# A fused patch-matching block and 5x5 convolution on one core: row tiles with the row slot outermost, and transposes one turn later

## The chip, the core and the metric

The kernel runs on one core of a Trainium2 chip. A core has a matrix engine (TensorE, PE in the profile; its weight loads are listed apart as PEld), a vector engine (VectorE, DVE), an activation engine (ScalarE, ACT), a general engine (GpSimd, POOL) and a synchronising engine (SyncE, SP) that here only issues transfers. Sixteen DMA engines move data between the on-chip memory (SBUF, 128 partitions) and the chip's main memory, or within SBUF. TensorE writes its sums to PSUM, a small memory of its own. The metric is the device time of one execution in microseconds (us), the median over several executions.

## The reference

The input x has shape 8 x 32 x 128 x 128 (images, channels, rows, columns), all float32. Layer 0 normalises x over 16 groups of channels, matches patches, and runs three rounds of a 1x1 and a depthwise 3x3 convolution over 256 channels; its result is added to x. Layer 1 normalises again and adds a 5x5 convolution of each channel with one kernel.

```python
xb = _patch_match_stack(x)            # the 8 best of 25 shifts per pixel: 32*8 = 256 channels
dct = _conv(xb, dct_w, groups=C)
h = relu(_conv(_conv(xb, w1), w2, groups=CK, pad=1))
h = relu(_conv(_conv(h, w3), w4, groups=CK, pad=1))
wiener = sigmoid(_conv(_conv(h, w5), w6, groups=CK, pad=1))
filt = _conv(wiener * dct, inv_dct_w, groups=C)
return _conv(filt, agg_w)
...
x = x + _L0_conv_ref(_gn(x), ...)
x = x + _L1_conv_ref(_gn(x), L1_conv_kernel, 1, 2)
```

## The kernel before

An image is cut into 16 strips of 8 rows, and one more step flushes the last rows, so the main loop has 17 steps for each of 8 images. A step has four turns, for i = 3, 2, 1, 0. In turn i = 1, 2 or 3, round i of the convolutions handles the strip that has come down to it; turn 0 multiplies by the dct and starts the final sums. Every turn also gathers one unit (a half width of four rows) of the stack of matched pixels: two activations build masks (sel, L616 and L617) from the indices (ib), and TensorE picks the pixels (pg, L631).

The 256 channels are split in two halves of 128. For the second half the 1x1 convolution (`pointwise_v`, pv, L670) goes to the tile tv by ACT (L678), and the depthwise 3x3 is done tap by tap: ACT does the first (L721), DVE the other eight (L724). For the first half, `pointwise_t` (p, L694) writes to the row tile t through ACT copies (L701), and `depthwise_t` (pw, L750) does the 3x3 on TensorE. To use more of the matrix rows, t holds several rows of the strip side by side in the partitions: four groups of 32 partitions are four rows, four channel groups q lie along the free dimension, and four slots hold rows at different shifts. Slots 2 and 3 are what `pointwise_t` wrote, rows 0 to 3 and 4 to 7. Slots 0 and 1 are the same rows moved by 64 partitions, and need transfers within SBUF, the doubling transfers, issued by SP: L706 copies slots 2 and 3 of the lower 64 partitions to slots 0 and 1 of the upper ones, L708 copies slot 2 of the upper ones to slot 1 of the lower, and after the depthwise step `rows_before_t` (L648) saves slot 3 of the upper partitions as slot 0 of the lower for the next strip. In turn i, p and the transfers L706 and L708 of round i come first, and the depthwise pw of round i follows in the next turn. tv has a similar transfer (L655).

The next image is prepared beside all this, in small tasks. A task is a generator that yields the name of a queue (D for work on DVE, A for ACT, P for TensorE, Q for the squares' sums), a cost, and optionally a number of turns to wait. `push` (L211) puts it in its queue with the earliest turn at which it may run; `run` (L217) runs, in the order of the queue, what is due. `now` counts turns: it is raised in `tick` (L1016), which runs the D queue up to a credit. In each turn of the main loop the order is: the pv matmuls; in turn 3 the final sums pa (L830) of the turn before; `run("P")` (L1083); in turn 0 the dct (`final_dct`, pc, and the DVE products L817, which free pc's PSUM tiles); `run("Q")`; `tick` (L1091); the second part of the final sums on DVE (L838); the eight taps; p with its transfers; pg; pw; `run("A")`.

Three tasks matter here. `costs` (L485) sums the squared differences of a quarter of the image's rows on DVE (L508 to L520, first the tile v, then dsum), transposes them on TensorE (pt, L525), and finds the eight best (L536, L537). `places` (L542) then turns the indices of the quarter into places in a table on DVE (oc, L551 to L560), yields "P" (L566), transposes them on TensorE (pi, L569), casts them on ACT (li, L571) and writes them out with four POOL transfers (idxd, L573). v (L505) and oc (L548) share one buffer: both have the tag "v" with bufs=1. An image has four quarters, i = 0 to 3.

PE, DVE and ACT run in the order in which the program is written; the order on SP and POOL, which issue the transfers, is set by a planner with a cost model.

Of the kernel before, what the change touches and what calls it, by code (L numbers as in the profile page):

```python
# [16 lines left out]
P = 128  # L17
C, K, H, W = 32, 8, 128, 128
# [26 lines left out]
def bm3d_conv_preact(  # L45
# [16 lines left out]
    nc = tc.nc  # L62
# [54 lines left out]
    tb = [const.tile([P, 4, 4, W], F32, name=f"t{i}") for i in range(3)]  # L117
# [367 lines left out]
    def costs(b, i, sq, idx):  # L485
# [35 lines left out]
        for h in range(0, R, 4):  # L521
# [9 lines left out]
            for q in range(4):  # L531
                yield "D", 1.85
                y = 8 * i + h + q
                for rg in range(4):
# [3 lines left out]
                        idx[:, rg, y // 4, :, y % 4], mx[:, 4 * q + rg], c25  # L538
                    )
        push(places(b, idx, i))  # L540

    def places(b, idx, i):  # L542


        if i == 0:
            idxd[b] = dram.tile([4, 8, 2, K * 4, HW], U8, name=f"idxd_{b}", tag="idxd")
        yield "D", 2.6
        oc = work.tile([P, R, W + 2], F32, name=f"oc_{b}_{i}", tag="v", bufs=1)  # L548
        oc = oc.rearrange("p r w -> p (r w)")
        o, ct = oc[:, 0:256], oc[:, 256:512]  # L550
        nc.vector.tensor_copy(  # L551
            o.rearrange("p (g z) -> p g z", g=4),
            idx[:, :, 2 * i : 2 * i + 2].rearrange("p g s k y -> p g (s k y)"),
        )
        nc.vector.tensor_scalar(ct, o, 5.0, None, op0=ALU.is_ge)
        for lim in (10.0, 15.0, 20.0):
            nc.vector.scalar_tensor_tensor(ct, o, lim, ct, op0=ALU.is_ge, op1=ALU.add)
        nc.vector.scalar_tensor_tensor(o, ct, float(QW - 5), o, op0=ALU.mult, op1=ALU.add)
        o3 = o.rearrange("p (s y) -> p s y", y=4)
        nc.vector.tensor_tensor(  # L560
            o3,
            o3,
            base.unsqueeze(1).to_broadcast([P, 64, 4]),
            ALU.add,
        )
        yield "P", 0  # L566
        for h in range(2):
            pt = ps_x.tile([P, 512], F32, name=f"pi_{b}_{i}_{h}", tag="x")
            nc.tensor.transpose(pt[:, :P], o[:, h * P : (h + 1) * P], ident)  # L569
            li = work.tile([P, P], U8, name=f"li_{b}_{i}_{h}", tag="li")  # L570
            nc.scalar.copy(li, pt[:, :P])  # L571
            for f in range(2):
                nc.gpsimd.dma_start(  # L573
                    idxd[b][i, 4 * h : 4 * h + 4, f],
                    li[:, HW * f : HW * (f + 1)],
                )
        ready.add((b, i))
        if i == 3:
            ready.add(b)
# [64 lines left out]
    def rows_before_t(i, b, n):  # L644

        t = tb[i - 1]
        if n < NS:
            nc.sync.dma_start(t[0:64, :, 0], t[64:P, :, 3])  # L648
        else:
            nc.gpsimd.memset(t[0:64, :, 0], 0.0)  # L650

    def rows_before_v(i, b, n):
        v = tv[i - 1]
# [26 lines left out]
    def pointwise_t(i, b, n, lhsT, src):  # L680
        t = tb[i - 1]
        nb = 2 if n < NS else 1
        nr = 4 if n < NS else i - 1
        if n == NS and i == 1:
            nc.gpsimd.memset(t[:, :, 2], 0.0)
        else:
            for q in range(2):
                ps = ps_x.tile([P, 2, 2, W], F32, name=f"p{i}_{b}_{n}_{q}", tag="x")
                for e in range(2):
                    s = slice(C * (2 * q + e), C * (2 * q + e + 1))  # L690
                    for g in range(2):
                        rows = src(g)
                        for r in range(nr):
                            nc.tensor.matmul(  # L694
                                ps[C * r : C * (r + 1), e, :nb],
                                lhsT[:, g, s],
                                rows[:, r : r + 4 * nb - 3 : 4],
                                start=g == 0,
                                stop=g == 1,
                            )  # L700
                nc.scalar.copy(  # L701
                    t[: C * nr, 2 * q : 2 * q + 2, 2 : 2 + nb], ps[: C * nr, :, :nb]
                )
            for r in range(i - 1) if n == 0 else range(i - 1, 4) if n == NS else ():
                nc.gpsimd.memset(t[C * r : C * (r + 1), :, 2], 0.0)
        nc.sync.dma_start(t[64:P, :, 0:nb], t[0:64, :, 2 : 2 + nb])  # L706
        if nb == 2:
            nc.sync.dma_start(t[0:64, :, 1], t[64:P, :, 2])  # L708

    def depthwise_v(i, b, n):  # L710
        v = tv[i - 1]
# [18 lines left out]
        rows_before_v(i, b, n)  # L730

    def depthwise_t(i, b, n):
        t = tb[i - 1].rearrange("p q (h k) w -> p q h k w", k=2)
        nb = 2 if n < NS else 1

        pt = [
            ps_dw.tile([P, 2, 2, W], F32, name=f"pw{i}_{b}_{n}_{u}", tag=f"dw{u}")
            for u in range(2)
        ]

        nh = [2 if n < NS else (i + 1 - u) // 2 for u in range(2)]

        parts = ((1, 2), (0, 1)) if i != 2 and n < NS else ((0, 2),)
        for ka, kz in parts:
            for u in range(2):
                hi, kz = 96 if u == 0 else P, min(kz, nh[u])
                for dx in (0, -1, 1):
                    xa, xz = max(0, -dx), min(W, W - dx)
                    for j in range(4 if kz > ka else 0):
                        nc.tensor.matmul(  # L750
                            pt[u][C * j : C * (j + 1), ka:kz, :nb, xa:xz],
                            dwd[0:hi, i - 1, u, j, dx + 1],
                            t[0:hi, j, ka:kz, :nb, xa + dx : xz + dx],
                            start=dx == 0,
                            stop=True,
                            skip_group_check=True,
                        )
        yield 1
        acc = accp.tile([P, R, W], F32, name=f"acc{i}_{b}_{n}_0", tag=f"acc{i}0")
        rows = acc.rearrange("p (k e) w -> p e k w", e=4)  # L760
        for u in range(2):
            if nh[u]:
                nc.scalar.activation(  # L763
                    rows[:, u : u + 2 * nh[u] - 1 : 2, :nb], pt[u][:, : nh[u], :nb], funcs[i - 1]
                )
        rows_before_t(i, b, n)
        accs[i, b, n][0] = acc

# [265 lines left out]
    with tc.manual_schedule(engines=ORDERED):  # L1034
# [2 lines left out]
        push(mixes())  # L1037
        xbd[0] = dram.tile([P, 2, H, W], F32, name="xbd_0", tag="xbd")
        for i in range(3):
            nc.gpsimd.memset(tb[i][0:64, :, 0], 0.0)  # L1040
        for u in range(7):
            unit(gather_load, u)

# [10 lines left out]
        for s in range(len(steps) + 2):  # L1054
            if s < len(steps):
                b, n = steps[s]
# [8 lines left out]
            for i in (3, 2, 1, 0):  # L1065
# [6 lines left out]
                if live and i:  # L1072
                    src = source(i, bi, ni)
                    pointwise_v(i, bi, ni, lws[i - 1], src)
                    new_v, new_t = depthwise_v(i, bi, ni), depthwise_t(i, bi, ni)
                    accs[i, bi, ni] = [None, next(new_v)]
# [17 lines left out]
                if live and i:  # L1094
                    pointwise_t(i, bi, ni, lws[i - 1], src)
# [81 lines left out]
```

## Time and profile before

| | |
|---|---|
| median of 3 runs | 6640.18 us (6636.07 to 6641.82) |
| the profiled execution | 6645.45 us, span 6643.7 us |
| PE busy, share of the span | 6238.3 us, 94% |
| DVE busy | 5862.9 us, 88% |
| ACT busy | 5054.4 us, 76% |
| POOL busy | 3079.3 us, 46% |
| queue 1 (transfers issued by SP): packets, MB, share of the 16 DMA engines | 383568, 258.11, 17.6% |
| queue 0 (transfers issued by POOL) | 383648, 611.87, 36.9% |
| L724 (DVE taps): count, mean | 3264, 1237 ns |
| L750 (pw on PE): count, mean | 31680, 420 ns |
| granted TensorE clock, mean | 0.978 |

The profile is of one execution; its span runs from the first to the last instruction. A line of the list of waits reads: engine, tile and line that waited, what ended the wait, then the total in us, the number of waits and the longest. A line of the timeline reads: start in us, length in us, engine, line, operation, tiles written and read with their sizes, how many such instructions are merged, and in brackets the idle time of that engine just before and what ended it. A wait for several things is put down to the one that came last by the profile, which can be an unrelated transfer. Matmuls overlap, so a TensorE line's length is not a sum of its instructions' lengths.

### The profile page before, as it was taken

What the parts mean: (1) busy time and instruction counts of PE and PEld (TensorE: products, weight loads), DVE (VectorE), ACT (ScalarE), POOL (GpSimd) and SP (SyncE); (2) the same over time, 40 slices, a digit from 0 to 9 for tenths busy, and PEclk for the clock granted to TensorE, in tenths of its full rate; (3) what the DMA queues carried; (4) which work ended last, traced back from release to release, by engine and by line L of the source; (5) the groups of instructions that cost most, each with busy time, mean ns of one, the idle gap of its engine ahead of it and who ended that gap; (6) DMA issues with size and microseconds to landing.
All of it is one profiled execution on the core that took longest, in us unless ns stands there. A gap on an engine that the chain in (4) does not pass through costs nothing.

```text
span 6643.7 us, 234197 instructions
## 1 busy us (share of the span) xinstructions
PE 6238.3 (94%) x102306; PEld 3236.5 (49%) x102306; DVE 5862.9 (88%) x8828; ACT 5054.4 (76%) x6698; POOL 3079.3 (46%) x5015
## 2 busy tenths in 40 slices
PE   5898899999999999999999999999999999999997
PEld 1444455544555545544555544554445544454553
DVE  7889988999889998898989998899888999887786
ACT  5787778777787777877778877887769777687772
POOL 8354346444464343643446444464435543344334
PEclk8899999999999999999999999999999999999998
DMA  4555555656555564655646656465555655556553
GB/s 85 126 138 130 131 131 130 148 134 140 131 143 136 130 147 118 149 134 133 144 121 147 147 126 149 120 154 136 130 137 132 148 136 130 125 141 145 137 133 82
DMA packets 770751, 886.20 MB, mean 133 GB/s; under 512 B 248880, under 2 KB 614000, under 8 KB 769728
## 3 DMA queue, kind: packets, MB, share of 16 engines
q0 software_dynamic: 383648, 611.87, 36.9%
q1 hardware_dynamic: 383568, 258.11, 17.6%
q8 instruction: 805, 13.19, 0.9%
q10 hardware_dynamic: 2512, 1.25, 0.1%
q14 instruction: 218, 1.79, 0.1%
HBM read 420.60 MB, written 216.49 MB: 96 GB/s over the span
## 4 chain that ended last, share of the span: by engine, by line
PE 43%; DVE 29%; DMA 9%; ACT 8%; POOL 6%; issue 4%; SPq 0%; ACTq 0%; DVEq 0%; POOLq 0%
DVE acc L724 20%; PE pw L750 14%; PE pv L670 11%; PE p L694 9%; PE pg L631 3%; DMA t<-t 3%; POOL xtd L424 2%; DVE df L444 2%; DVE idx L537 2%; PE pc L809 2%; ACT sel L616 2%; ACT df L452 2%; DMA xf<-xbd 2%; DVE acc L817 1%; PE p L923 1%
## 5 line engine op out<-in xcount | busy, mean ns | idle before, releaser
L724 DVE SCALAR_TENSOR_TENSOR acc<-tv,dwv,acc 128x1024 f32<-128x1024 f32 (+3 forms) x3264 | 4032.3, 1237 | 240.8 <-ACT acc L721 136.8
L750 PE MATMUL pw<-t,dwd 96*32 96x254 f32 (+7 forms) x31680 | 2124.6, 420 | 51.0 <-DMA t<-t 38.4
L750 PEld LDWEIGHTS pw<-t,dwd 96*32 96x32 f32 (+1 forms) x31680 | 1088.4, 110 | 874.5 <-issue 411.2
L616 ACT ACTIVATE sel<-ib,nplace 128x1024 f32<-128x1024 uint8 x1024 | 1172.1, 1145 | 37.4 <-DMA ib<-idxd 37.4
L617 ACT ACTIVATE sel<-sel 128x1024 f32<-128x1024 f32 x1024 | 1085.7, 1060 | 32.5
L694 PE MATMUL p<-acc,lw 128*32 128x256 f32 x16768 | 1002.9, 383 | 24.7 <-ACT tv L678 23.3
L670 PE MATMUL pv<-acc,lw 128*32 128x512 f32 x8448 | 956.2, 590 | 48.7 <-DVE acc L817 43.4
L602 POOL DMA_DIRECT2D ib<-idxd x512 | 292.5, 571 | 1241.8 <-ACT sel L616 1176.2
L790 POOL DMA_DIRECT2D xf<-xbd x1088 | 651.9, 631 | 316.1 <-PE pc L809 180.1
L694 PEld LDWEIGHTS p<-acc,lw 128*32 128x32 f32 x16768 | 579.2, 111 | 437.1 <-issue 79.4
L452 ACT ACTIVATE df<-df 128x786 f32<-128x786 f32 (+2 forms) x576 | 468.6, 861 | 340.5 <-DVE df L444 337.8
L631 PE MATMUL pg<-sel,xt 120*32 120x88 f32 (+1 forms) x24576 | 616.1, 244 | 63.6 <-ACT sel L617 50.7
L631 PEld LDWEIGHTS pg<-sel,xt 120*32 120x32 f32 x24576 | 556.8, 110 | 235.0 <-ACT sel L617 70.1
L678 ACT COPY tv<-pv 128x512 f32<-128x512 f32 (+2 forms) x784 | 437.1, 579 | 305.0 <-PE pv L670 293.0
L444 DVE TENSOR_TENSOR df<-xn 128x786 f32<-128x786 f32 (+2 forms) x576 | 531.6, 973 | 81.2 <-PE pd L459 80.2
L728 ACT ACTIVATE acc<-acc 128x1024 f32<-128x1024 f32 (+3 forms) x408 | 417.3, 1023 | 241.6 <-DVE acc L724 241.3
L763 ACT ACTIVATE acc<-pw 128x512 f32<-128x512 f32 (+2 forms) x808 | 438.5, 573 | 182.7 <-PE pw L750 182.0
L670 PEld LDWEIGHTS pv<-acc,lw 128*32 128x32 f32 x8448 | 286.0, 111 | 534.1 <-issue 428.7
L701 ACT COPY t<-p 128x512 f32<-128x512 f32 x800 | 424.4, 571 | 118.0 <-PE p L694 118.0
L721 ACT ACTIVATE acc<-tv,dwv 128x1024 f32<-128x1024 f32 (+3 forms) x408 | 454.9, 1115 | 33.9 <-PE pa L830 20.6
L670 PE MATMUL pv<-xb,lw 128*32 128x512 f32 x4096 | 473.5, 596 | 0.0
L694 PE MATMUL p<-xb,lw 128*32 128x256 f32 x8192 | 468.5, 379 | 1.0 <-DVE xy L935 0.9
(155 smaller groups left out, 5932.9 us busy)
## 6 DMA issues: line engine op xcount, KB each, us to landing
ib<-idxd POOLq DMA_DIRECT2D x512, 256.0 KB, 4.1
xbd<-xb POOLq DMA_DIRECT2D x128, 1024.0 KB, 5.9
xf<-xbd POOLq DMA_DIRECT2D x960, 128.0 KB, 7.1
t<-t SPq DMA_DIRECT2D x792, 128.0 KB
t<-t SPq DMA_DIRECT2D x384, 256.0 KB
tv<-tv SPq DMA_DIRECT2D x384, 130.0 KB
xt<-xtd POOLq DMA_DIRECT2D x240, 180.0 KB, 3.7
xtd<-xl POOLq DMA_DIRECT2D x192, 96.0 KB, 3.5
```

The lines of the kernel that those rows point to most:

```text
L444: nc.vector.tensor_sub(df[:, :, ca:cz], xn[:, r0 : r0 + SR, ca:cz], xn[:, r0 + dy : r0 + dy + SR, ca + dx : cz + dx],)
L452: nc.scalar.activation(df[:, :, ca:cz], df[:, :, ca:cz], AF.Square)
L616: nc.scalar.activation(sel, ib, AF.Square, bias=nplace)
L617: nc.scalar.activation(sel, sel, AF.Relu, scale=-1.0, bias=1.0)
L631: nc.tensor.matmul(pg[C * j : C * (j + 1), :, :, xa:xz], xt[: 8 * QW, f * (NT // 2) + t], sels[j // 2][: 8 * QW, j % 2 * 2 : j % 2 * 2 + 2 ...
L670: nc.tensor.matmul(ps[C * j : C * (j + 1), :hr], lhsT[:, g, P + C * j : P + C * (j + 1)], src(g)[:, h : h + hr], start=g == 0, stop=g == 1,)
L694: nc.tensor.matmul(ps[C * r : C * (r + 1), e, :nb], lhsT[:, g, s], rows[:, r : r + 4 * nb - 3 : 4], start=g == 0, stop=g == 1,)
L721: nc.scalar.activation(acc, rows, AF.Copy, scale=tap)
L724: nc.vector.scalar_tensor_tensor(acc, rows, tap, acc, op0=ALU.mult, op1=ALU.add)
L750: nc.tensor.matmul(pt[u][C * j : C * (j + 1), ka:kz, :nb, xa:xz], dwd[0:hi, i - 1, u, j, dx + 1], t[0:hi, j, ka:kz, :nb, xa + dx : xz + dx ...
L763: nc.scalar.activation(rows[:, u : u + 2 * nh[u] - 1 : 2, :nb], pt[u][:, : nh[u], :nb], funcs[i - 1])
L790: nc.gpsimd.dma_start(xf[p : p + C, m, j0:j1], src[g, m, (h + m + 1) % 2, :, :, ya:yz])
```

## The change

In the row tiles t the slot becomes the outermost of the free dimensions: from (q, slot, column) to (slot, q, column). All accesses to t follow. What a doubling transfer moves in one partition was four pieces of one or two rows (512 or 1024 bytes) and is now one piece of four or eight rows (2048 or 4096 bytes). A depthwise matmul that takes two or four rows of one q now finds them 512 elements apart instead of 128. Apart from that, the P part of `places` waits one more turn for every image but the first.

```diff
@@ places
-        yield "P", 0
+        yield "P", 0, 1 if b else 0
@@ rows_before_t
-            nc.sync.dma_start(t[0:64, :, 0], t[64:P, :, 3])
+            nc.sync.dma_start(t[0:64, 0], t[64:P, 3])
         else:
-            nc.gpsimd.memset(t[0:64, :, 0], 0.0)
+            nc.gpsimd.memset(t[0:64, 0], 0.0)
@@ pointwise_t
-            nc.gpsimd.memset(t[:, :, 2], 0.0)
+            nc.gpsimd.memset(t[:, 2], 0.0)
...
                 nc.scalar.copy(
-                    t[: C * nr, 2 * q : 2 * q + 2, 2 : 2 + nb], ps[: C * nr, :, :nb]
+                    t[: C * nr, 2 : 2 + nb, 2 * q : 2 * q + 2].rearrange("p b e w -> p e b w"),
+                    ps[: C * nr, :, :nb],
                 )
...
-                nc.gpsimd.memset(t[C * r : C * (r + 1), :, 2], 0.0)
-        nc.sync.dma_start(t[64:P, :, 0:nb], t[0:64, :, 2 : 2 + nb])
+                nc.gpsimd.memset(t[C * r : C * (r + 1), 2], 0.0)
+        nc.sync.dma_start(t[64:P, 0:nb], t[0:64, 2 : 2 + nb])
         if nb == 2:
-            nc.sync.dma_start(t[0:64, :, 1], t[64:P, :, 2])
+            nc.sync.dma_start(t[0:64, 1], t[64:P, 2])
@@ depthwise_t
-        t = tb[i - 1].rearrange("p q (h k) w -> p q h k w", k=2)
+        t = tb[i - 1].rearrange("p (h k) q w -> p q h k w", k=2)
@@ before the first step
-            nc.gpsimd.memset(tb[i][0:64, :, 0], 0.0)
+            nc.gpsimd.memset(tb[i][0:64, 0], 0.0)
```

## The prediction

> **What bounds the kernel now.** I read the page first, then the waits of TensorE, the instructions that touch tile v, and the timeline around the work that moves.
>
> ```profile
> span 6643.7 us, 234197 instructions
> ...
> PE 6238.3 (94%) x102306; PEld 3236.5 (49%) x102306; DVE 5862.9 (88%) x8828; ACT 5054.4 (76%) x6698; POOL 3079.3 (46%) x5015
> ...
> PE 43%; DVE 29%; DMA 9%; ACT 8%; POOL 6%; issue 4%; SPq 0%; ACTq 0%; DVEq 0%; POOLq 0%
> ```
>
> Two engines share the bound: PE idles only 405 us, and DVE holds 29% of the chain. Which one binds changes from step to step, so each edit must be priced where it falls. The waits of PE hold both stalls that the change touches:
>
> ```profile
> PE pi L569 <- DVE oc L560: 63.2, 16, 20.2
> ...
> PE pv L670 <- DVE acc L817: 43.4, 25, 3.0
> PE pw L750 <- DMA t<-t: 38.4, 27, 4.0
> ```
>
> The moved transposes (pi) cost 63.2 us in 16 waits, the doubling transfers 38.4 us in 27. The question is what stands behind each. Tile v, which shares its single buffer with oc, gives the first hint, in the list of what DVE waited for:
>
> ```profile
>   PE pi L569: 2.8, 4
> ```
>
> **Part 1, the transposes one turn later.** P items run before the tick of a turn. An item left by tick N runs now in turn N+1, before tick N+1; with the extra turn it runs in turn N+2, after tick N+1. Image 0 keeps the old order; its four waits (1.2, 6.8, 20.2, 8.1) are 36.3 of the 63.2 us. What is left is 26.9: 2.0, 8.6 and 3.1 in image 1, about 2.1 in each of the six last quarters of images 2 to 7 (12.4), and 0.8 in small ones.
>
> The last quarters are worth nothing. In the timeline, during image 4, for image 5:
>
> ```profile
> 4082.96 0.42 DVE L560 TENSOR_TENSOR oc<-oc,base 128x256 f32<-128x256 f32 x1
> 4083.30 10.52 DVE L724 SCALAR_TENSOR_TENSOR acc<-tv,dwv,acc 128x1024 f32<-128x1024 f32 x8
> 4083.53 0.41 PE L569 MATMUL pi<-cst,oc 128*128 128x128 f32 x2 [2.14 <-DVE oc L560]
> ...
> 4093.74 2.47 DVE L817 TENSOR_TENSOR acc<-acc,pc 128x512 f32<-128x512 f32 x4
> 4094.47 5.34 PE L670 MATMUL pv<-acc,lw 128*32 128x512 f32 x32 [2.20 <-DVE acc L817]
> ```
>
> DVE goes from oc through eight taps to L817 without a gap, and PE waits for L817 again 11 us later. PE that skips the first 2.1 us waits 2.1 more at the second: 0 of 12.4.
>
> The third quarters turn into a loss, and it is the largest term. Quarter 2 of images 2 to 7 (and quarter 1 of image 1) has the costs of the next quarter (L508, tile v) in tick N+1, directly behind oc on DVE:
>
> ```profile
> 4003.40 0.43 DVE L560 TENSOR_TENSOR oc<-oc,base 128x256 f32<-128x256 f32 x1
> ...
> 4003.99 0.44 PE L569 MATMUL pi<-cst,oc 128*128 128x128 f32 x2
> ...
> 4004.46 1.24 DVE L508 TENSOR_TENSOR v<-dsum 128x1040 f32<-128x1040 f32 x1 [0.64 <-DMA xf<-xbd]
> ...
> 4008.41 1.23 DVE L520 TENSOR_TENSOR dsum<-dsum,v 128x1024 f32<-128x1024 f32 x1
> ...
> 4012.34 0.66 PE L525 MATMUL pt<-cst,dsum 128*128 128x128 f32 x4
> ```
>
> ```profile
> 4809.37 1.24 DVE L508 TENSOR_TENSOR v<-dsum 128x1040 f32<-128x1040 f32 x1 [0.59 <-PE pi L569]
> ```
>
> L508 starts 0.03 us after the second transpose ends (here, and in the next image, where the idle time is put down to pi): v may not overwrite oc before the transposes have read it. After the change those transposes stand in turn N+2, where L525 stands now. Per case: 4012.34 less the 0.37 us that pi gives up at its old place is 4011.97; the transposes end at 4012.41, L508 starts at 4012.44 instead of 4004.46. DVE is 7.98 us late. The other five images give the same to 0.02 us (the distances from L508 to L525 are all 7.86 to 7.88). PE stalls too: L525 needs L520, which ends 5.2 us after L508's start, so PE stands 5.2 us at L525. Behind L508 on DVE are L838 and the three runs of eight taps of that step, and none has slack: after 4004.46 the next idle time of DVE over 0.15 us comes at 4051.99, past L817 at 4045.08, for which PE waits 0.7 us (1.1, 1.8, 1.0, 1.4 and 2.0 in the others). So the whole 8.0 reaches PE: 6 x 8.0 = +47.8 us. The least would be PE's own stall, 6 x 5.2 = 31, if DVE caught up.
>
> Image 1: quarter 1 loses 6.0 us on DVE (L508 from 711.92 to 717.95), quarter 2's wait of 8.6 goes, quarter 3's 3.1 falls before a stretch in which DVE runs 30 us without a gap. DVE next idles 6.6 us in that stretch at 822. So of +6.0 and -8.6, between -1 and +5 is left; I take +2. Quarters 0 and 1 of images 2 to 7 have 53 us or more until the next v: 0. With the transposes go two li casts (0.21 us each; ACT is 76% busy) and four idxd issues (0.69 us each) on POOL, which waits 160 us for li now, with xf, ib and sq issues behind; those are loaded turns ahead, and idxd is read a quarter later, at least a step away. I put 0, and 10 us to either side.
>
> **Part 2, the layout.** Instructions on PE, ACT and POOL are as many as before. A depthwise row now lies 512 elements from the next. L694 reads rows at that distance already: 64 instructions over 256 columns issue in 3.45 us, 54 ns each; L750's 96 over 254 or 256 take 5.16, also 54 ns. Cost 0. The L701 copies write four runs instead of two, as L678 does: 579 against 571 ns, 800 times, 6 us on ACT, hidden by its 24% idle time; on the path it would be those 6. The memsets (about 0.52 us) become contiguous: 0.
>
> The transfers carry the same bytes in a quarter of the pieces: L708 and L648 64 x 2 KB instead of 256 x 512 B, L706 64 x 4 KB instead of 256 x 1 KB. From the recorded completions, issue end to last completion, median and 90th percentile:
>
> | line | pieces | us |
> |---|---|---|
> | L706 | 256 x 1024 B | 3.40, 7.31 |
> | L648 | 256 x 512 B | 3.24, 7.48 |
> | L708 | 256 x 512 B, behind L706 | 3.61, 7.42 |
> | L655 (tv) | 128 x 1040 B | 2.73, 6.48 |
>
> Twice the bytes in as many pieces cost nothing in the tail; half the pieces with the same bytes save 0.9. So the tail goes by pieces. The PE waits are L708's slowest: landing 10 to 14 us after issue in most of them, PE arriving 1 to 3 us earlier. At 2022 to 2034 L706's and L708's pieces trickle in beside an out_dram transfer that lands in 11 us, 1 KB pieces taking 106 to 158 ns (76 is their median) between 4 KB packets of some 400. A quarter of the pieces should bring these landings below 9 us. Addressable: 38.4, and the 3.1 that the view puts down to tv; less 2.6 in four waits with an L817 wait right behind; less 3.4 of the very last (4.0 us, only 3.5 after an issue); less 3.5 in five steps where DVE is soon the later one: 32. I take 85%: -27. Ends: +3 (bytes decide; 4 KB pieces hold up others, though 121,696 such packets run already) and -39.
>
> The Trainium skill (DMA: Bandwidth & Descriptors, Why small descriptors are slow) holds the penalty of small pieces to be one of HBM, not of SBUF to SBUF. By it part 2 is worth 0 and the sum is +50. The tv row says otherwise in the tail, by 0.9 us.
>
> Fewer pieces also free DMA time: q1's t packets take 14.5% of the 16 engines now. For other loads I put -2.
>
> **Sum**, against the profiled run (span 6643.7, device time 6645.5, which is 5.3 above the median of 6640.2): 47.8 + 2 - 27 - 2 = +21. Median 6661.
>
> **Rivals.**
> A. DVE's wait at v does not reach the end: PE, not DVE, is the later one there, or v's order differs. For: DVE's share is 88%, not 100. Against: no gap in DVE until L817, and PE waits there in all six. It ends faster once over 27 of the 48 us is hidden; with all hidden 6640 - 27 - 5 (image 1's wait) - 2 = 6606. Chance 0.15.
> B. The transfers land no sooner. For: an L706 piece of 1 KB takes 76 ns, tv's 1040 B 47, so bytes may bind with 64 partitions. Against: the tails above. 6640 + 50 = 6690. Chance 0.15.
> C. SP and POOL, whose order a planner sets from its own costs, are ordered differently, and xf or ib come late. Against: PE has no wait for xf. Some 15 us either way about the sum, 6645 to 6676. Chance 0.10.
>
> **How the numbers follow.** My forecast has 0.60; its own range is 6643 to 6685 (part 1 between 31 + 2 and 53, part 2 between -10 and -29). The 8 in 10 range, 6612 to 6692, takes in most of A and B. A measurement of this kernel can tell about 0.2% (13 us) from no change. Faster: 0.13 of A, 0.02 of C, 0.01 of mine, 0.16. Same: 0.16 of mine, 0.02 of A, 0.03 of C, 0.21. Slower: 0.43 of mine, all of B, 0.05 of C, 0.63.
>
> **What the profile after would show.** Part 1: DVE v L508 waiting for PE pi seven times, some 55 us in all; PE pt L525 waiting about 5 us six times for DVE dsum; PE pi's wait down to the 36 us of image 0; L817 waits of 2 to 3 us at the end of those steps. Part 2: PE pw waiting for t<-t under 10 us; t<-t as 2 and 4 KB pieces; L694 and L750 at 54 ns. I am wrong if L508 still starts within a microsecond of oc's end, or if pw's wait stays above 25 us.

## The result, and the profile after

| | before | after |
|---|---|---|
| median | 6641.44 us (6636.07 to 6652.68, 5 runs) | 6671.53 us (6665.80 to 6675.45, 5 runs) |
| ratio to before, 95% interval | | 1.0044 [1.0029, 1.0059] |
| profiled execution, span | 6643.7 us | 6673.7 us |

The change makes the kernel 0.44% slower, about 29 us. The forecast was 6661 us, slower. Lines of the code after L701 are one higher than before (L724 is now L725, L750 is L751, L817 is L818, L708 is L709).

The page of the kernel after. The first lines are the span and the busy times; then the queue that SP feeds (packets, MB, share of the 16 DMA engines), and the chain by engine:

```profile
span 6673.7 us, 234198 instructions
...
PE 6246.8 (94%) x102306; PEld 3230.4 (48%) x102306; DVE 5862.1 (88%) x8828; ACT 5051.2 (76%) x6698; POOL 3081.1 (46%) x5015
...
q1 hardware_dynamic: 157776, 258.11, 15.9%
...
PE 46%; DVE 27%; ACT 10%; DMA 7%; POOL 6%; issue 4%; SPq 0%; ACTq 0%; POOLq 0%; DVEq 0%
```

No engine does more work than before: the counts in the line of busy times are the same. SP's queue carries the same 258.11 MB in 157,776 packets instead of 383,568. Of the 30 us of span, 21.5 are idle time of PE (405.4 us before, 426.9 after), and 8.5 are the same matmuls taking longer (6238.3 us before, 6246.8 after). The list of waits of PE after the change says which waits are new:

```profile
PE pg L631 <- ACT sel L617: 63.0, 39, 2.3
...
PE pt L525 <- issue: 37.2, 8, 5.3
PE pi L569 <- DVE oc L560: 36.0, 4, 20.3
PE pw L751 <- DMA t<-t: 22.7, 17, 3.9
```

The wait for oc fell from 63.2 us to the 36.0 of image 0, and the wait for the doubling transfers from 38.4 to 22.7. In their place PE stands 37.2 us at pt, which was not in the list of before in this size, and 12 us more than before at pg, whose wait for sel was 50.7 us. The wait at pt is put down to "issue", that is to nothing the profile shows; the timeline below shows what it is. The list of waits of DVE after the change has one new row:

```profile
DVE v L508 <- PE pi L569: 53.9, 8, 8.1
```

It was 2.8 us before. The timeline of the kernel after, around quarter 2 of an image, the same place as the one shown for before at 4003 us:

```profile
4020.84 0.42 DVE L560 TENSOR_TENSOR oc<-oc,base 128x256 f32<-128x256 f32 x1
...
4028.75 0.44 PE L569 MATMUL pi<-cst,oc 128*128 128x128 f32 x2
...
4029.22 1.24 DVE L508 TENSOR_TENSOR v<-dsum 128x1040 f32<-128x1040 f32 x1 [7.96 <-PE pi L569]
...
4033.17 1.23 DVE L520 TENSOR_TENSOR dsum<-dsum,v 128x1024 f32<-128x1024 f32 x1
...
4034.49 1.08 PE L525 MATMUL pt<-cst,dsum 128*128 128x128 f32 x4 [5.31 <-issue]
...
4035.51 5.18 PE L694 MATMUL p<-acc,lw 128*32 128x256 f32 x64
```

Read it from the top. oc is complete at 4021.26. The transposes that read it now start 7.49 us later. v may not be written before they are done, because it lies in the same buffer, so DVE idles 7.96 us and starts L508 0.03 us after the transposes' end. L520 ends at 4034.40, and the pt transposes, which need its result, start 0.09 us later: the 5.31 us that are put down to "issue" end with dsum. Both numbers were in the forecast: 7.98 and 5.2.

The last line shows where PE's longer busy time comes from. The same 64 matmuls took 3.66 us behind the transposes of before:

```profile
4004.36 3.66 PE L694 MATMUL p<-acc,lw 128*32 128x256 f32 x64
```

In the trace the granted clock is 0.50 from 4031.8 to 4038.6 us, and 1.00 in the 11.8 us before. Each of the other five stalls of 5.3 us at pt has 6.8 us at 0.50 around its end too, in the kernel after and in e1 and e8 below. So each of the six costs PE its 5.3 us and, by the lengths of L525 (1.08 against 0.66 us) and L694, an estimated 1.9 us more here; where L694 takes 5.65 and 5.75 us, at two other stalls, it is 2.4 and 2.5.

### The profile page after: what moved, and what is told of

It is laid out like the page before. It is cut to its first block, busy times and chain, and to the rows that moved or that the text cites. A ratio compares the mean times of both kernels' runs of the same rounds, so it can differ in the third digit from the quotient of the medians.

```text
span 6673.7 us, 234198 instructions
## 1 busy us (share of the span) xinstructions
PE 6246.8 (94%) x102306; PEld 3230.4 (48%) x102306; DVE 5862.1 (88%) x8828; ACT 5051.2 (76%) x6698; POOL 3081.1 (46%) x5015
## 3 DMA queue, kind: packets, MB, share of 16 engines
q1 hardware_dynamic: 157776, 258.11, 15.9%
## 4 chain that ended last, share of the span: by engine, by line
PE 46%; DVE 27%; ACT 10%; DMA 7%; POOL 6%; issue 4%; SPq 0%; ACTq 0%; POOLq 0%; DVEq 0%
DVE acc L725 19%; PE pw L751 16%; PE pv L670 12%; PE p L694 10%; PE pg L631 4%; POOL xtd L424 3%; ACT sel L616 2%; DVE idx L537 2%; PE pc L810 2%; DMA t<-t 2%; ACT df L452 2%; DVE df L444 2%; PE pa L831 1%; DMA xf<-xbd 1%; DVE acc L818 1%
## 5 line engine op out<-in xcount | busy, mean ns | idle before, releaser
L725 DVE SCALAR_TENSOR_TENSOR acc<-tv,dwv,acc 128x1024 f32<-128x1024 f32 (+3 forms) x3264 | 4032.1, 1237 | 248.1 <-ACT acc L722 144.0
L751 PE MATMUL pw<-t,dwd 128*32 128x254 f32 (+7 forms) x31680 | 2124.6, 420 | 30.1 <-DMA t<-t 22.7
L751 PEld LDWEIGHTS pw<-t,dwd 128*32 128x32 f32 (+1 forms) x31680 | 1089.4, 111 | 854.2 <-issue 403.8
L616 ACT ACTIVATE sel<-ib,nplace 128x1024 f32<-128x1024 uint8 x1024 | 1172.4, 1145 | 34.2 <-DMA ib<-idxd 34.2
L694 PE MATMUL p<-acc,lw 128*32 128x256 f32 x16768 | 1011.3, 384 | 20.6 <-ACT tv L678 19.6
L694 PEld LDWEIGHTS p<-acc,lw 128*32 128x32 f32 x16768 | 578.0, 112 | 436.3 <-issue 81.6
L701 ACT COPY t<-p 128x512 f32<-128x512 f32 x800 | 424.1, 571 | 125.0 <-PE p L694 125.0
L694 PE MATMUL p<-xb,lw 128*32 128x256 f32 x8192 | 468.3, 380 | 3.7 <-ACT tv L678 3.7
```

The lines of the kernel that those rows point to most:

```text
L616: nc.scalar.activation(sel, ib, AF.Square, bias=nplace)
L694: nc.tensor.matmul(ps[C * r : C * (r + 1), e, :nb], lhsT[:, g, s], rows[:, r : r + 4 * nb - 3 : 4], start=g == 0, stop=g == 1,)
L725: nc.vector.scalar_tensor_tensor(acc, rows, tap, acc, op0=ALU.mult, op1=ALU.add)
L751: nc.tensor.matmul(pt[u][C * j : C * (j + 1), ka:kz, :nb, xa:xz], dwd[0:hi, i - 1, u, j, dx + 1], t[0:hi, j, ka:kz, :nb, xa + dx : xz + dx ...
```

## The experiments

Each median is of 5 to 12 executions. The ratio is to the kernel before, with its 95% interval; one per cent is 66 us.

| kernel | layout | delay | oc | out_dram pieces | median us | ratio |
|---|---|---|---|---|---|---|
| after | new | yes | shares v's | 62 rows | 6671.53 | 1.0044 [1.0029, 1.0059] |
| e8 | new | yes | shares v's | 62 | 6674.56 | 1.0041 [1.0029, 1.0053] |
| e1 | old | yes | shares v's | 62 | 6679.61 | 1.0045 [1.0030, 1.0060] |
| e2 | new | no | shares v's | 62 | 6628.55 | 0.9971 [0.9961, 0.9980] |
| e3 | new | yes | its own | 62 | 6622.37 | 0.9961 [0.9946, 0.9975] |
| e4 | new | no | its own | 62 | 6622.27 | 0.9960 [0.9946, 0.9974] |
| e11 | old | yes | its own | 62 | 6629.39 | 0.9979 [0.9968, 0.9989] |
| e5 | new, without L709 | no | shares v's | 62 | 6619.75 | 0.9955 [0.9942, 0.9968] |
| e6 | new | no | shares v's | 32 + 30 | 6602.40 | 0.9934 [0.9921, 0.9947] |
| e7 | old | no | shares v's | 32 + 30 | 6610.77 | 0.9948 [0.9935, 0.9961] |
| e9 | new | no | its own | 32 + 30 | 6604.33 | 0.9940 [0.9927, 0.9953] |
| e10 | new | yes | its own | 32 + 30 | 6603.18 | 0.9940 [0.9927, 0.9952] |

### Each part alone (e1, e2)

e1 keeps the old layout and has only the delay:

```diff
-        yield "P", 0
+        yield "P", 0, 1 if b else 0
```

> The row tiles as before, only the transposes of places one turn later. Theory (v waits in the shared buffer for the transposes): +46 us on the time before, ratio about 1.007; DVE v L508 waits some 54 us for PE pi, PE pt L525 some 5 us in seven places, PE pw waits for t<-t about 38 us as before. Rival (the layout costs the time, the delay is harmless or helps): ratio 1.000 or below, no wait of v.

e2 is the kernel after with that one line undone.

> The new layout alone, transposes where they were. Theory: 10 to 20 us faster than before, ratio 0.997 to 0.9985, since PE pw's wait for t<-t fell from 38 to 23 us in the changed kernel; v waits under 4 us. Rival (the layout costs): ratio about 1.004, like the changed kernel. Rival (the landings are worth nothing): 1.000.

Measured: the delay alone costs 0.45% (30 us) where 46 were expected, the layout alone gains 0.29% (19 us). The wait at v in e1's list of waits of DVE, and the answering ones in its list of PE:

```profile
DVE v L508 <- PE pi L569: 57.6, 8, 8.2
```

```profile
PE pw L750 <- DMA t<-t: 42.4, 27, 4.4
...
PE pt L525 <- issue: 37.0, 7, 5.3
PE pi L569 <- DVE oc L560: 36.9, 4, 20.2
```

In e2, v waits for pi only 2.9 us in all, and in its list of PE's waits the doubling transfers stand at what they are in the kernel after:

```profile
PE pi L569 <- DVE oc L560: 62.1, 13, 20.2
...
PE pw L751 <- DMA t<-t: 20.7, 16, 3.9
```

So the loss is the delay's, and the layout is a gain. But the two do not add: 30 less 19 would be +11, and the kernel after has +0.44% and, run again as e8, +0.41%, the same as the delay alone. Read the other way, the delay costs 0.70 to 0.73% (46 to 48 us) on top of the new layout, and 0.45% on top of the old. These two differ by some 18 us, little more than their uncertainty of about 15.

### Is it the shared buffer? (e3, e11, e4)

The rival to the hold at v is that the later transposes, casts and transfers of places cost the time themselves. e3 leaves the delay and the order of all work as in the kernel after, and gives oc a buffer of its own, so v no longer has to wait:

```diff
-        oc = work.tile([P, R, W + 2], F32, name=f"oc_{b}_{i}", tag="v", bufs=1)
-        oc = oc.rearrange("p r w -> p (r w)")
+        oc = work.tile([P, 512], F32, name=f"oc_{b}_{i}", tag="oc", bufs=1)
```

> The whole change, but oc has a buffer of its own, so v need not wait for the transposes. Theory: v's 54 us of waits and the 5 us waits of pt go, the time is 15 to 22 us below that of before, ratio 0.9967 to 0.998. Rival (the later transposes cost through POOL's idxd transfers or ACT's casts, not through the buffer): the time stays with the changed kernel's, ratio about 1.004.

The timeline of e3 at the same place as the one above:

```profile
3993.30 0.42 DVE L559 TENSOR_TENSOR oc<-oc,base 128x256 f32<-128x256 f32 x1
3993.67 1.24 DVE L508 TENSOR_TENSOR v<-dsum 128x1040 f32<-128x1040 f32 x1
...
4001.08 0.44 PE L568 MATMUL pi<-cst,oc 128*128 128x128 f32 x2
...
4001.35 0.60 PE L525 MATMUL pt<-cst,dsum 128*128 128x128 f32 x4
```

The transposes are as late as in the kernel after (7.36 us behind oc's end; 7.49 there), but v follows oc without a gap, pt follows pi without one, and these waits of v and pt are gone from the lists. The ratio goes from 1.0044 to 0.9961: 0.83%, 55 us, taken back by a buffer alone, and somewhat more than expected. e11 is the same pair with the old layout (e1 with oc's own buffer):

> Old layout, delay, oc in a buffer of its own: the delay without its price, and a second measure of the layout, against the kernel with new layout, delay and own buffer (0.9961). Theory (the layout is worth 0.25 to 0.3% wherever v is not held): ratio 0.9985 to 1.000. Rival (the layout is worth nothing beside the delay, as the 1.0041 and 1.0045 of the two delayed kernels suggest): 0.996 to 0.997.

From e1 to e11 it is 0.66%, 44 us, with e11 a little under its expected range. These differences carry some 12 to 14 us of uncertainty each. That the hold at v is the loss is shown; that the transposes' lateness itself costs nothing shows in e4, which has the own buffer and no delay:

> New layout and oc's own buffer, transposes where they were. Tells what the delay by itself is worth once v cannot be held. Theory (PE's waits for oc in the last quarters only move to the next wait for DVE): within 8 us of the kernel with own buffer and delay, ratio 0.997 to 0.9985. Rival (the 27 us of waits that the delay takes away are worth their length): 25 us slower than that kernel, ratio about 1.001.

e3 and e4 have the same time (0.9961 and 0.9960). PE waits 36.8 us for oc in the one and 62.0 in the other, and the 25 us between them are worth nothing: where PE skips that wait it meets a later one. Its idle time in all is no less in e3, 403.5 us against 396.6; its waits at pd for df are 53.6 us against 44.2, and at pv for L817 47.5 against 39.7. The own buffer without the delay (e2 to e4) gains 0.11%, 6 to 7 us, within the uncertainty; that part of e3's 55 us may be due to the buffer and not to the hold.

### What the doubling transfers can be worth, and what makes them late (e5, e6, e7)

e5 is e2 without the transfer L709. Slot 1 of the lower partitions stays zero, so the rows that the depthwise step reads there are left out of the sums; the number of matmuls is unchanged.

```diff
         nc.sync.dma_start(t[64:P, 0:nb], t[0:64, 2 : 2 + nb])
-        if nb == 2:
-            nc.sync.dma_start(t[0:64, 1], t[64:P, 2])
...
-            nc.gpsimd.memset(tb[i][0:64, 0], 0.0)
+            nc.gpsimd.memset(tb[i][0:64, 0:2], 0.0)
```

> New layout, transposes where they were, and the transfer of L709 (slot 2 of the upper partitions to slot 1 of the lower) left out, so that rows 2 and 3 of the lower groups are zero: what the doubling transfers can bring at most. Theory (what is left of PE pw's wait for t<-t, 20 us, is nearly all L709): that wait under 5 us, 12 to 18 us faster than the layout alone, ratio 0.994 to 0.9955. Rival (PE only waits elsewhere): ratio as the layout alone, 0.997.

Measured 0.9955, with PE's wait for these transfers almost gone:

```profile
PE pw L749 <- DMA t<-t: 4.9, 3, 4.0
```

That bounds it: of the 20.7 us that e2 still waits, taking the later transfer away altogether brings 0.16%, 10 us, and the intervals of the two overlap.

Most of the waits that remain after the change have one thing in common in the trace: beside 11 of the 17, and 15.9 of the 22.7 us, transfers of 62 output rows, out_dram<-xy, were issued. The other six have none near them. At 3665.3 us, for example, L709 was issued 13.12 us before PE's wait ends and landed 0.04 us before that, when 15 of its 16 completions had been in for 2.1 us; an out_dram transfer was issued 13.24 us before and landed 0.13 us after. Those land in 11 us, and unevenly: of the 16 completions of each, the first comes 5.1 us after the issue, the eighth 6.1, the last 11.4 (medians). e6 is e2 with those transfers cut in two, and e7 is the kernel before with the same cut:

```diff
-                for a, z in ((0, 62), (66, P)):
+                for a, z in ((0, 32), (32, 62), (66, 96), (96, P)):
```

> New layout, transposes where they were, and each output transfer of 62 rows cut in one of 32 and one of 30. Theory (the late landings of t come from the one or two DMA engines on which a 62-row transfer, 11 us to landing, ends long after the other engines): out_dram<-xy lands in 5 us or less, PE pw's wait for t<-t falls from 20 to under 8 us, ratio 0.993 to 0.996. Rival (the queues are simply full): the wait stays near 20 us, ratio 0.997 or more, since POOL issues 112 transfers more.

> The kernel before with the output transfers cut in the same way, rows of t in pieces of 512 and 1024 bytes as before. Theory (uneven engines): PE pw's wait for t<-t falls from 38 to 42 us to under 12 with the old pieces, ratio 0.994 to 0.997. Rival (the number of pieces makes the waits): the wait stays above 30 us, ratio 0.999 to 1.002.

In e2, everything about out_dram, columns: shortest, median and longest of one issue on POOL in ns, then first and last start; then who on POOL waited for those transfers, and issue to landing:

```profile
L938 POOL DMA_DIRECT2D out_dram<-xy x112: 1504/1519/1587, 1210.7 to 6154.7; - x112
...
L938 POOL DMA_DIRECT2D out_dram<-xo x8: 1502/1504/1546, 6583.8 to 6606.0; - x8
...
  POOL xy L885: 105.4, 15
  POOL xf L791: 85.4, 50
  POOL xy L890: 42.4, 14
...
DMA to landing us min/median/max: 1.9/10.8/16.2
```

The same of e6:

```profile
L938 POOL DMA_DIRECT2D out_dram<-xy x224: 561/588/637, 1210.1 to 6152.8; - x112
...
L938 POOL DMA_DIRECT2D out_dram<-xo x16: 565/583/623, 6579.0 to 6599.0; - x16
...
  POOL xy L890: 28.1, 13
  POOL xy L885: 2.5, 2
...
DMA to landing us min/median/max: 1.6/2.2/5.2
```

A part lands in 2.2 us where the whole took 10.8 (medians over all output transfers), and takes POOL 0.59 us to issue instead of 1.52. POOL itself waited 233 us for them in those three rows of e2, and waits 31 in e6. PE's wait for the doubling transfers in e6, and then in e7, which has the old small pieces:

```profile
PE pw L751 <- DMA t<-t: 8.8, 7, 3.7
```

```profile
PE pw L750 <- DMA t<-t: 16.3, 14, 4.1
```

| PE's wait at pw, us | 62 rows | 32 + 30 rows |
|---|---|---|
| old layout | 38.4 | 16.3 |
| new layout | 20.7 | 8.8 |

One profile is not exact here: the other kernels with 62 rows have 40.2 and 42.4 with the old layout and 19.2 to 26.6 with the new, and those with 32 + 30 rows and the new layout 8.3 and 10.8. The cut brought the two waits down a little less than expected (under 12 with the old layout, under 8 with the new). The landings agree: the 90th percentile of L708, from the issue's end to the last completion, is 7.42 us before, 5.62 with the cut alone (e7) and 7.16 with the layout alone (L709 in e2). So the landings were late in good part because of these output transfers, and the layout and the cut take the same waits from two sides. With the old layout the cut gains 0.52%, with the new one 0.37% more (0.9971 to 0.9934); the layout on top of the cut is worth 0.14% (0.9948 to 0.9934), half of its 0.29% alone, and the intervals of that pair overlap. Part of the cut's gain is no matter of t at all: the kernel ends with such transfers. From the start of the last issue of this line to the end of the span it takes 17.4 us in e2 (6606.0 to 6623.4) and 6.1 in e6 (6599.0 to 6605.1), 11.3 us less.

e6 has the lowest ratio of this study: 0.66% faster than before, and 1.1% faster than the change.

### The delay once more, with all of this gone (e9, e10)

e9 is e6 with oc's own buffer, e10 is e9 with the delay.

> Everything that helped, without the delay: new layout, output transfers cut in 32 and 30 rows, oc in a buffer of its own. Theory: the own buffer alone brings under 8 us, so ratio 0.992 to 0.9935, the fastest of all. Rival (the own buffer moves other things for the worse): 0.994 or more.

> The same with the transposes one turn later. Theory (with v free the delay neither helps nor harms, as between the two kernels with own buffer): within 8 us of the kernel without the delay, ratio 0.991 to 0.9945. Rival (the delay takes away 25 us of waits that count once the transfers are out of the way): 0.989.

Both come to 0.9940, and e6 without either to 0.9934, all within the uncertainty. The delay is worth nothing even where it harms nothing, and so is the buffer, to which e9's expectation had given up to 8 us.

> The changed kernel again, beside the others, since the delay alone came out as slow as the whole change. Theory (the parts add up, +0.45% and -0.29%): ratio 1.001 to 1.003. Rival (the layout is worth nothing once v is held): 1.0045 as at first.

e8, the kernel after on the chip of e5 to e7, gave 1.0041; v waited 54.9 us for pi in its profile. So the parts do not add here either, and the loss repeats.

## Why the prediction was right or wrong

**The sum** was +21 us, measured about +29, inside the forecast's own range. Its main mechanism is shown. That the number came so near is in part luck: the layout brought less than forecast, and the delay alone cost less too, so that two errors offset each other; and the sum took for granted that the two parts add, which they do not.

**The hold at v** (+47.8, and +6 in image 1, if all of it reaches the end): v waited 53.9 us in 8 places where seven and some 55 were forecast (the eighth, 0.84 us in image 0, stands before as well), 7.96 us in the one shown against 7.98 worked out, PE 5.31 at pt against 5.2. It reaches the end in full, or nearly: e3 takes back 55 us, e11 44, of which the buffer by itself may be worth some 6. Rival A, in which it did not, is out. The prediction has no term for the clock, which stands at 0.50 for 6.8 us at each of the six stalls. With it PE's own loss is an estimated 7.2 to 7.8 us at each (5.3 standing, 1.9 to 2.5 on slower matmuls) and not the 5.2 that made its low end of 31 us; how much of the 8 us comes by DVE and how much by PE is not separated.

**Image 1 and the last quarters.** The last quarters were put at 0, since DVE sets their end, and they are. The timeline of the kernel after, one quarter on:

```profile
4107.55 0.42 DVE L560 TENSOR_TENSOR oc<-oc,base 128x256 f32<-128x256 f32 x1
4107.89 10.52 DVE L725 SCALAR_TENSOR_TENSOR acc<-tv,dwv,acc 128x1024 f32<-128x1024 f32 x8
...
4118.33 2.47 DVE L818 TENSOR_TENSOR acc<-acc,pc 128x512 f32<-128x512 f32 x4
...
4119.06 1.92 PE L670 MATMUL pv<-acc,lw 128*32 128x512 f32 x16 [2.65 <-DVE acc L818]
```

One wait of 2.65 us stands where there were 2.14 and 2.20, and from oc's end to the matmuls behind L818 it is 11.09 us as before (4083.38 to 4094.47 there): nothing gained.

**The net of the delay** was forecast at some 50 us. On top of the new layout it cost 46 to 48, as forecast; alone it cost 30 (e1). If that difference is real, a gain is missing from the forecast, and the term that would have to hold it is "Quarters 0 and 1 of images 2 to 7 have 53 us or more until the next v: 0". In quarter 1 of the image shown, PE waited 0.21 us for oc, 1.28 for df and 3.67 for tv (p, L694) before the change, and 0.59 for df and 1.96 for tv after it, about 2 us less. Why is not shown. The own buffer with the delay and the old layout (e11) ends 14 us under the kernel before, which has the same sign, but no run tells the buffer's share there from the delay's; with the new layout and the own buffer the delay is worth nothing (e3 against e4). The cause of the 18 us stays open.

**Part 2** (-27, ends +3 and -39) was over-sized. The step that failed is the 85%: it took the tail of the landings to go by the number of pieces. The 1 KB pieces of 106 to 158 ns that it named at 2022 to 2034 us are the slow ones: by the packets on record half of the 1 KB pieces in that stretch took 66 ns or less. From the recorded completions, issue end to last completion, median, 90th and 97th percentile:

| transfer | before | after |
|---|---|---|
| L706, now L707 | 3.40, 7.31, 9.81 | 3.07, 7.14, 8.78 |
| L708, now L709 | 3.61, 7.42, 9.28 | 3.50, 6.96, 8.69 |
| L648 | 3.24, 7.48, 8.28 | 3.42, 6.89, 7.76 |

A quarter of the pieces took 0.2 to 0.6 us from the 90th percentile and 0.5 to 1.0 from the 97th. The slowest landings, for which PE waits, still come late: pw's wait went to 22.7 us instead of under 10. It did not stay above the 25 that was to refute the step, though in e3 it is 26.6. What made most of these landings late stood beside them in the trace, the output transfers of 62 rows (e6 and e7). The worth of the layout is 19 us alone, 0.18% (12 us) between e11 and e3, 0.14% between e7 and e6, and 1 to 3 us beside the delay. Between 0 and 20, then, and why it is least there is open. One way would be that PE, let through earlier at pw, waits for a DVE that the hold has made late; no run separates that from the uncertainty of these differences.

The page of the Trainium skill that the prediction set against the tv row (DMA: Bandwidth & Descriptors, Why small descriptors are slow) came closer than the prediction did: between parts of SBUF, pieces four times as large moved the median landing by 0.3 us at most. It isn't nothing, though: alone the layout gains 0.29% [0.20, 0.39]. So rival B, no gain from it, is out for the layout by itself, and near the truth beside the delay with the shared buffer.

What was costed at nothing stayed there: L751 and L694 issue a matmul per 54 ns in both layouts, and an L701 copy takes 571 ns in both, so the 6 us that were feared on ACT did not come. Rival C, late loads, does not show: PE has no wait for xf in its list, and ACT waits 34.2 us for ib after the change and 37.4 before it.

## What to carry to other kernels

Before a reader is moved later, look up who writes its buffer next: two tiles under one tag with a single buffer turned a free delay into 8 us of DVE, six times over, and a buffer of its own removed it. Look at the granted clock behind a new stall as well: here 5.3 us of standing came with 6.8 us at half the clock. A wait in a list is worth only what stands behind it: 25 us of waits for oc went away from e4 to e3 for no gain, while an own buffer for a wait that the list of before showed at 2.8 us decided the sign. When transfers land late, look at what else was issued in those microseconds before reshaping the transfers that are late; the list of POOL's waits of before had named it:

```profile
POOL xf L790 <- DMA out_dram<-xy: 83.3, 49, 4.4
```

Forty-nine times a load stood behind an output transfer.

## What was not expected of the hardware

A transfer of 62 partitions from SBUF to the main memory, 4 pieces of 512 bytes each, costs far more than two of 32 and 30: 1.52 us against 0.57 and 0.60 to issue on POOL, 11 us against 2.1 and 2.4 to land (e2 and e6). The queue that POOL feeds shows a difference in packets, in the pages of the kernel before and of e6 (packets, MB, share of the 16 DMA engines):

```profile
q0 software_dynamic: 383648, 611.87, 36.9%
```

```profile
q0 software_dynamic: 357024, 611.00, 36.3%
```

The same output takes 26,624 packets less, 208 for each of the 128 transfers. By the sizes in the trace they are small: packets of 32 bytes fall from 31,488 to 4,736, those of 16 bytes from 1,792 to none. They come on top of the output, since the queue moves 0.88 MB less for the same result. The trace doesn't say what they carry, and whether these packets or POOL's longer issue delay the other transfers was not separated.

The Trainium skill advises against cutting a transfer by partitions (DMA: Bandwidth & Descriptors, Rules for kernel authors): two transfers over disjoint halves of the partitions share the same engines and serialize, so that one transfer over all 128 should be used. For 62 partitions the measurement decides otherwise: e7 is 0.52% [0.39, 0.65] faster than the kernel before by this cut alone. For transfers of 128 partitions no run here says anything.
